# A two-layer vision block: fc1 by blocks of quarters, convolution taps cut to the image, and w1's sums kept in banks

## The chip, the cores and the metric

The kernel runs on one core of a Trainium2 chip. The metric is the device time of one execution in microseconds; the kernel before has a median of 3316.8 us in three runs (3315.48 to 3319.44). The core has a matrix engine (TensorE, PE in the profile), a vector engine (VectorE, DVE), a scalar engine (ScalarE, ACT), and GpSimd (POOL), which here mostly issues DMAs that add to memory. PE writes its results to eight banks of an accumulator memory (PSUM), each of 128 partitions by 512 fp32 numbers. DVE and ACT read them from there.

## The reference

The input is eight images of 384 channels by 32 x 32 points, all in fp32. Two layers follow.

```python
# layer 0: attention and MLP over the 1024 points of an image
xn = layernorm(x); q, k, v = split(xn @ w_qkv.T + b_qkv)
x1 = softmax(q @ k.T * SCALE) @ v @ w_proj.T + b_proj + x
h = gelu(layernorm(x1) @ w_fc1.T + b_fc1)          # 384 -> 1536: "fc1"
y = x1 + h @ w_fc2.T + b_fc2                       # 1536 -> 384: "fc2"
# layer 1: ConvNeXt block with global response normalization
z = depthwise_conv_7x7(y, dw_w, padding=3)         # 49 taps a channel
z = gelu(layernorm(z) @ w1 + b1)                   # 384 -> 1536: "up"
z = z * (1 + gamma * norm_over_points(z) / mean_over_channels(...)) + beta
out = y + z @ w2 + b2                              # 1536 -> 384: "down"
```

## The kernel before

An image is held as channels on 128 partitions, three tiles deep, by 1024 points in two halves of 512. A product is one weight tile of 128 x 128 times 512 points. The order of instructions is made by a small model of PE's time, `flow`: every product calls `flow.pe(U)` with `U = 0.857`, and chains of other work (norms, the convolution) are generators whose `yield` says after how many microseconds of PE time their next piece is emitted. The order on each engine is thus fixed when the program is built; at run time each engine goes through its own list and waits on semaphores.

Several layers already use schemes of the Strassen kind: fc2 and w2 in thirds with 15 products for 18, q/k and w1 with 11 for 12. fc1 is plain:

```python
def gelu_half(hid, m, h, xn, weights, wname, name):
    w = weights.at(wname, m // CM)[:, m % CM * CT : (m % CM + 1) * CT, :]
    ps = linear_half(lambda k: w[:, k, :], lambda k: xn[:, k, :], CT, h, f"{name}_{h}_{m}")   # 3 products
    other_table(hid[:, m, half(h)], ps, AF.Gelu, bias=bfc1[:, m : m + 1])

def mlp(...):
    for m in range(HT):                      # HT = 12 output tiles, first half of the points
        gelu_half(hid, m, 0, xn, weights, wa, f"fc1_{b}")
        if m == 3 and rest:
            rest()                           # second half of proj
            ln = flow.spawn(layernorm(xt, xn, 1, eps0, "g2", f"ln2_{b}", True, slow=slow))
            behind_ln(ln)                    # norm after the convolution of the image before
    flow.finish(ln)
    for m in range(HT):                      # second half of the points
        gelu_half(hid, m, 1, xn, weights, wa, f"fc1_{b}")
        ...
```

The convolution of image b-1 goes on while image b is in its attention and fc1. DVE makes 42 of the 49 taps of each channel tile over a padded image, always 32 x 32; ACT multiplies the other seven and POOL's DMA adds them:

```python
while min(done) < taps:
    ...
    dy, dx = divmod(i, KS)
    window = pad[:, ct, dy + y0 : dy + y1, dx : dx + W]
    dst = image(acc[:, ct, :])[:, y0:y1, :]
    nc.vector.scalar_tensor_tensor(dst, window, tap, dst, ALU.mult, ALU.add)     # L980
    ...
    yield next((early for m, early in first if n <= m), us)
```

In the last image the last convolution has nothing of a next image to hide in. It goes over rows in two parts, into `wqkv` (its lines are L980 too). The norms of each convolution subtract the mean (L423) from a bank that PE has filled with sums.

The w1 stage makes two output tiles at a time. Each product or pair goes into a bank of its own, and DVE adds the banks up in SBUF (L1051):

```python
nc.scalar.copy(c21, product((a11, b11)))
plus(c11, product((a13, b31), (a12, b21)), c21)
accumulate(p5, [(s1, t1)])
plus(c21, product((s2, t2)), c21)
plus(c12, p5, c21)
plus(c12, product((s4, b22), (a13, b32)), c12)
finish(i)                                    # gelu
plus(c21, product((s3, t3)), c21)
plus(c22, p5, c21)
plus(c21, product((a23, b31), (a22, t4)), c21)
plus(c22, product((a23, b32)), c22)
```

The sums of weights that these schemes need are made once, beside image 0, by a chain `prepare`: POOL's queue loads blocks into the tile that is later `acc`, DVE adds them, POOL's queue stores the forms in HBM. The same queue carries the folds of the norms (L388), by which half of the partitions are added to the other half before PE sums the rest (L394).

Of the kernel before, what the change touches and what calls it, by code (L numbers as in the profile page):

```python
# [51 lines left out]
P = 128  # L52
# [12 lines left out]
CM = 2  # L65
NC = HT // CM
U = 0.857
HELPED = 7
SCALE = HD ** -0.5
EPS0, EPS1, GRN_EPS = 1e-5, 1e-6, 1e-6  # L70
# [81 lines left out]
def block_kernel(  # L152
# [25 lines left out]
    flow = Flow()  # L178
    quiet = []
    s_fc2 = dram.tile([P, len(FORMS), 4 * P], F32, tag="s_fc2", bufs=1, name="s_fc2")  # L180
    s_w2 = dram.tile([P, len(FORMS), 4 * P], F32, tag="s_w2", bufs=1, name="s_w2")
    s_qk = dram.tile([P, CT, 4 * P], F32, tag="s_qk", bufs=1, name="s_qk")
    s_w1 = dram.tile([P, HT // 2, 4, P], F32, tag="s_w1", bufs=1, name="s_w1")

    def half(h):
        return slice(h * NH, (h + 1) * NH)
# [106 lines left out]

    RAW = ("A11", "A12", "A21", "A22", "A31", "A32")

    def plan_fc1(tag):
        return [((f"fc1_{tag}", c), chunk(wfc1, c)) for c in range(NC)]

    def plan_fc2(tag):
        return [((f"fc2_{tag}", a), chunk(wfc2, c)) for c, a in enumerate(RAW)]  # L300
# [491 lines left out]
    def add_first(xt, r, n, bank):  # L792
        dst = xt[:, r, half(n)]
        nc.vector.scalar_tensor_tensor(dst, bank, col("bfc2", r), dst, ALU.add, ALU.add)  # L794

    def mlp(b, xt, xn, weights, tag, ln, rest, before_fc2=None, behind_ln=None):

        hid = one.tile([P, HT * N], F32, tag="big", name=f"hid_{b}").rearrange("p (m n) -> p m n", m=HT)
        e = [three.tile([P, 2, NH], F32, tag="p", name=f"fc2_e_{b}_{i}") for i in range(2)]
        wa = f"fc1_{tag}"  # L800
        flow.finish(ln)
        for m in range(HT):
            gelu_half(hid, m, 0, xn, weights, wa, f"fc1_{b}")
            if m == 3 and rest:
                rest()
                slow = 1.2 if b == 1 else 1.0
                ln = flow.spawn(layernorm(xt, xn, 1, eps0, "g2", f"ln2_{b}", True, slow=slow))
                behind_ln(ln)
        flow.finish(ln)
        for m in range(HT):  # L810
            gelu_half(hid, m, 1, xn, weights, wa, f"fc1_{b}")
            if m % CM == CM - 1:
                weights.used(wa, m // CM)
            if m in (3, 5):
                two_tiles = hid[:, m - 3 : m - 1, :]
                difference(e[(m - 3) // 2], two_tiles[:, :, half(0)], two_tiles[:, :, half(1)])
        if before_fc2:
            before_fc2()
        bias = lambda r: col("bfc2", r)
        by_thirds(xt, hid, e, True, weights, f"fc2_{tag}", bias, lambda r, n: pad_half(xt, r, n), f"fc2_{b}")  # L820
# [132 lines left out]
    def keep(b, xt):  # L953
# [2 lines left out]
        nc.sync.dma_start(out=kept.rearrange("(c p) n -> p c n", p=P), in_=xt)  # L956
        return kept

    def convolution(acc, us, first=(), y0=0, y1=H, ready=tuple(range(CT)), taken=None):

        done = [0] * CT
        ct, n = None, 0
        taps = KS * KS - (HELPED if taken is not None else 0)
        while min(done) < taps:
            left = [c for c in ready if done[c] < taps and not (taken and taken.get(c, 0) > flow.now)]
            if not left:
                yield 1.0
                continue  # L970
            ct = min([c for c in left if c != ct] or left, key=lambda c: done[c])
            i = done[ct]
            dy, dx = divmod(i, KS)
            window = pad[:, ct, dy + y0 : dy + y1, dx : dx + W]
            dst = image(acc[:, ct, :])[:, y0:y1, :]
            tap = col("dww", ct * KS * KS + i)
            if i == 0:
                nc.vector.tensor_scalar(dst, window, tap, col("dwb", ct), ALU.mult, ALU.add)  # L978
            else:
                nc.vector.scalar_tensor_tensor(dst, window, tap, dst, ALU.mult, ALU.add)  # L980
            done[ct] += 1
            n += 1
            yield next((early for m, early in first if n <= m), us)

    def help_convolution(acc, us, taken):

        yield 8.0
        for ct in reversed(range(CT)):
            taken[ct] = float("inf")
            for i in range(KS * KS - HELPED, KS * KS):  # L990
                dy, dx = divmod(i, KS)
                for h in range(2):
                    if quiet:
                        while quiet:
                            yield 1.0
                        yield 3.0
                    t = three.tile([P, NH], F32, tag="res", bufs=4, name=f"tap_{ct}_{i}_{h}")
                    y0 = dy + h * H // 2
                    window = pad[:, ct, y0 : y0 + H // 2, dx : dx + W]
                    tap = col("dww", ct * KS * KS + i)  # L1000
                    nc.scalar.mul(t.rearrange("p (h w) -> p h w", w=W), window, tap)  # L1001
                    nc.gpsimd.dma_start(out=acc[:, ct, half(h)], in_=t, accum_op=ALU.add)  # L1002
                    yield us
            taken[ct] = flow.now + 8.0
        yield 8.0
        taken.clear()
# [10 lines left out]
    def grn_up(b, acc, weights, tag):  # L1017
# [7 lines left out]
        wa = f"w1_{tag}"  # L1025
        spent = {}

        def finish(m):
            other_table(y[:, m, :], y[:, m, :], AF.Gelu, bias=b1[:, m : m + 1])

        def squares(i):
            for m in (i, i + HT // 2):
# [3 lines left out]
        for i in range(HT // 2):  # L1036
            j = i + HT // 2
            raw, sums = weights.at(wa, i, "A"), weights.at(wa, i, "S")
            a11, a12, a13, a22, a23 = (raw[:, k, :] for k in range(5))
            s1, s2, s3, s4 = (sums[:, k, :] for k in range(4))  # L1040
            spent[i] = ps_s.tile([P, 2, NH], F32, tag="s", name=f"h_{b}_{i}_5")
            p5 = spent[i][:, 0, :]
            c11, c12, c21, c22 = (y[:, m, half(n)] for m in (i, j) for n in range(2))

            def product(*pairs):
                bank = o_tile(f"h_{b}_{i}")
                accumulate(bank, list(pairs))
                return bank

            def plus(dst, bank, part):  # L1050
                nc.vector.tensor_tensor(dst, bank, part, ALU.add)  # L1051

            nc.scalar.copy(c21, product((a11, b11)))
            if i:
                finish(j - 1)
                squares(i - 1)
            plus(c11, product((a13, b31), (a12, b21)), c21)
            accumulate(p5, [(s1, t1)])
            plus(c21, product((s2, t2)), c21)
            plus(c12, p5, c21)  # L1060
            plus(c12, product((s4, b22), (a13, b32)), c12)
            finish(i)
            plus(c21, product((s3, t3)), c21)
            plus(c22, p5, c21)
            plus(c21, product((a23, b31), (a22, t4)), c21)
            plus(c22, product((a23, b32)), c22)
            for part in ("A", "S"):
                weights.used(wa, i, part)
        finish(HT - 1)
        squares(HT // 2 - 1)  # L1070
        return y, gx
# [189 lines left out]
    def prepare(weights, aside):  # L1261
# [17 lines left out]
        def load_blocks(w, name, *which):  # L1279
            t = one.tile([P, CT, N], F32, tag="acc", name=name).rearrange("p c n -> p (c n)")  # L1280
            parts = []
            for j, (m, k) in enumerate(which):
                parts.append(t[:, j * 4 * P : (j + 1) * 4 * P])
                nc.gpsimd.dma_start(out=parts[j], in_=block_of(w, m, k))
            return parts

        def spare(name):
            return three.tile([P, NH], F32, tag="res", bufs=4, name=name)
# [5 lines left out]
            nc.vector.tensor_tensor(dst, x, y, ALU.add)  # L1294

        def forms(name, w, store):
            def keep_form(i, t):
                nc.gpsimd.dma_start(out=store[:, i, :], in_=t)

            a11, a12, a31, a33, a13, a23 = load_blocks(w, f"{name}_a", (1, 1), (1, 2), (3, 1), (3, 3), (1, 3), (2, 3))  # L1300
            x, y, z = (spare(f"{name}_{k}") for k in "xyz")
            yield 16.0
            add(a23, a23, a33)
            add(a11, a11, a12)
# [17 lines left out]
            keep_form(12, a12)  # L1322
            nc.vector.tensor_scalar(a23, a23, -1.0, None, ALU.mult)
            keep_form(14, a23)
            a21, a22, a31, a32, a33, a12 = load_blocks(w, f"{name}_b", (2, 1), (2, 2), (3, 1), (3, 2), (3, 3), (1, 2))
            x, y = spare(f"{name}_v"), spare(f"{name}_w")
            nc.gpsimd.dma_start(out=x, in_=block_of(w, 2, 3))
            yield 25.0
            add(x, x, a33)
            sub(y, a22, x)  # L1330
            keep_form(7, y)
# [70 lines left out]
        yield 4.0  # L1402
        for j, key in enumerate(order):
            nc.gpsimd.dma_start(out=s_w1[:, :, int(key[1]) - 1, :], in_=t[:, j])
        yield from shift_through_w2()
        yield from forms("w2", w2, s_w2)

    def first_values(xn):

# [10 lines left out]
    def main():  # L1420
# [17 lines left out]
        plan = plan_fc1(0) + plan_fc2_fast(0) + plan_qk(1)  # L1438
        for b in range(1, B):
            if b < B - 1:  # L1440
                plan += plan_fc1(b) + plan_fc2_fast(b)
            else:
                for h in range(2):
                    plan += plan_fc1(f"{b}_{h}") + plan_fc2(f"{b}_{h}")
# [80 lines left out]
        for b in range(B):  # L1525
# [22 lines left out]
            flow.finish(state["norm3"])  # L1548
            if b < B - 1:
                y, gx = grn_up(b - 1, acc, weights, b - 1)  # L1550
                start_conv(b, 1.65 if b == B - 2 else 1.7, (26, 2.2), (27, 9.0), (35, 4.4))
                scale = flow.spawn(grn_scale(b - 1, gx, weights, b - 1, y))
                next_values(b + 1)
                flow.finish(scale)
# [166 lines left out]
```

## Time and profile before

| | us | share of 3315.9 |
|---|---|---|
| PE busy | 3279.8 | 99% |
| DVE busy | 2511.5 | 76% |
| ACT busy | 1604.1 | 48% |
| POOL busy | 484.2 | 15% |
| first product of `v` starts | 16.5 | |
| image 3: attention and proj | 1169.1 to 1296.3 | |
| image 3: fc1 | 1296.2 to 1367.8 | |
| image 3: fc2 | 1368.7 to 1421.6 | |
| image 2's w1 | 1421.5 to 1480.7 | |

An image takes 400 us in the middle of the run. In the profile, a line such as `L351 PE MATMUL fc<-xn,fc 128*128 128x512 f32 x1152 | 504.0, 596` is a group: its line in the kernel, engine and operation, the tile written and those read, the shape, the count, and the busy time and mean ns of one. Each fp32 product is two records, so 1152 records are 576 products. After the second bar stands idle time of the engine just before the group and what ended most of it. In the list of waits a row names the engine and line that waited, the one waited for, and total, times and longest. In a timeline the first number is the start, the second the length, and the bracket the idle time before it.

### The profile page before, as it was taken

The page shows a single profiled execution, that of the slowest core. Times are in us where ns is not written, and L with a number is a line of the kernel's source. Part 1 is how long each engine was busy: PE and PEld are TensorE (multiplying, and loading weights), DVE is VectorE, ACT ScalarE, POOL GpSimd, SP SyncE. Part 2 cuts the span into 40 slices and gives each one's busy share as a digit, 9 for nine tenths or more (in the row PEclk, how much of TensorE's full clock was granted, in tenths as well). Part 3 has the DMA queues.
Part 4 walks back from the last instruction along what each step waited for, and adds up shares of the span by engine and source line. Part 5 has one row for each costly group of instructions (what it writes and reads, how often), then busy time and mean ns, then how long its engine had stood idle before and what let it go on. Part 6 is the DMA issues. An engine that isn't in the chain of part 4 may idle for free. (4 is left out here: it accounts for less than half of the span.)

```text
span 3315.9 us, 38765 instructions
## 1 busy us (share of the span) xinstructions
PE 3279.8 (99%) x14296; PEld 1415.0 (43%) x14296; DVE 2511.5 (76%) x3186; ACT 1604.1 (48%) x2194; POOL 484.2 (15%) x569
## 2 busy tenths in 40 slices
PE   8999999999999999999999999999999999999998
PEld 4344434443344433444344443444434443444455
DVE  4444897888867978679786798768886888879940
ACT  2542663447534375353652737526473355623541
POOL 2121210112110121101211022111220112100000
PEclk9999999999999999999999999999999999999999
DMA  5336732657244563537436373273742647333231
GB/s 197 112 106 147 150 68 71 156 115 150 56 104 135 137 127 58 131 106 172 84 58 148 103 187 70 58 179 84 175 78 50 180 106 160 63 74 89 69 95 43
DMA packets 199109, 368.73 MB, mean 111 GB/s; under 512 B 40768, under 2 KB 46784, under 8 KB 198528
## 3 DMA queue, kind: packets, MB, share of 16 engines
q0 software_dynamic: 80896, 158.63, 26.3%
q1 hardware_dynamic: 117728, 206.83, 20.7%
q8 instruction: 115, 1.88, 0.2%
q10 hardware_dynamic: 288, 0.71, 0.1%
q14 instruction: 82, 0.67, 0.1%
HBM read 187.03 MB, written 34.60 MB: 67 GB/s over the span
## 5 line engine op out<-in xcount | busy, mean ns | idle before, releaser
L980 DVE SCALAR_TENSOR_TENSOR acc<-pad,vec,acc 128x1024 f32<-128x1024 f32 x861 | 1069.3, 1276 | 20.1 <-DMA acc<-tap 15.5
L673 ACT ACTIVATE p<-s 128x1024 f32<-128x1024 f32 x512 | 523.8, 1023 | 278.5 <-PE s L664 270.1
L664 PE MATMUL s<-qk 48*64 48x512 f32 x4096 | 544.7, 593 | 0.8 <-ACT p L673 0.6
L684 PE MATMUL o<-p,v 64*64 64x512 f32 x4096 | 541.2, 591 | 0.0
L351 PE MATMUL fc<-xn,fc 128*128 128x512 f32 x1152 | 504.0, 596 | 4.8 <-DVE acc L423 4.8
L1002 POOL DMA_DIRECT2D acc<-tap x294 | 253.7, 884 | 1212.2 <-ACT tap L1001 747.9
L351 PEld LDWEIGHTS fc<-xn,fc 128*128 128x128 f32 x1152 | 219.2, 191 | 285.6 <-issue 275.7
L358 PE MATMUL fc_p<-hid,fc 128*128 128x512 f32 x728 | 318.6, 594 | 0.2 <-DMA hid<-hid 0.2
L370 ACT ACTIVATE hid<-fc,bfc_f 128x512 f32<-128x512 f32 x192 | 131.5, 686 | 348.0 <-PE fc L351 347.6
L684 PEld LDWEIGHTS o<-p,v 64*64 64x64 f32 x4096 | 165.5, 133 | 278.3 <-issue 266.7
L664 PEld LDWEIGHTS s<-qk 48*64 48x64 f32 x4096 | 161.2, 133 | 278.6 <-issue 220.5
L358 PE MATMUL o_p<-y,w 128*128 128x512 f32 x624 | 272.3, 593 | 0.0
L1051 DVE TENSOR_TENSOR y<-h,y 128x512 f32<-128x512 f32 x288 | 197.0, 690 | 90.8 <-PE h L358 76.2
L1001 ACT ACTIVATE tap<-pad,vec 128x512 f32<-128x512 f32 x294 | 210.9, 727 | 25.4 <-DMA acc<-tap 25.2
L358 PEld LDWEIGHTS fc_p<-hid,fc 128*128 128x128 f32 x728 | 137.2, 190 | 179.0 <-issue 166.5
L358 PE MATMUL h<-acc,w_A 128*128 128x512 f32 x432 | 207.3, 595 | 0.0
L980 DVE SCALAR_TENSOR_TENSOR wqkv<-pad,vec,wqkv 128x416 f32<-128x416 f32 (+1 forms) x288 | 193.5, 744 | 0.5
L358 PEld LDWEIGHTS o_p<-y,w 128*128 128x128 f32 x624 | 117.5, 190 | 150.6 <-issue 129.1
L790 ACT COPY pad<-x 128x512 f32<-128x512 f32 x48 | 30.2, 635 | 251.0 <-DVE x L856 187.0
L625 DVE TENSOR_TENSOR attn<-o,attn 128x512 f32<-128x512 f32 x64 | 44.1, 689 | 138.6 <-ACT attn L623 138.6
L549 DVE TENSOR_TENSOR qk<-qk,qk 128x512 f32<-128x512 f32 x168 | 111.5, 686 | 29.0 <-PE qk L358 20.0
L592 PE MATMUL v<-wqkv,xn 128*128 128x384 f32 x384 | 128.2, 491 | 0.0
(311 smaller groups left out, 3751.4 us busy)
## 6 DMA issues: line engine op xcount, KB each, us to landing
acc<-tap POOLq DMA_DIRECT2D x294, 256.0 KB, 3.5
w_A<-in_w SPq DMA_DIRECT2D x72, 384.0 KB
fc<-s_fc SPq DMA_DIRECT2D x91, 256.0 KB
hid<-hid POOLq DMA_DIRECT2D x42, 512.0 KB, 7.1
fc<-in_wfc SPq DMA_DIRECT2D x54, 384.0 KB
w<-s_w SPq DMA_DIRECT2D x78, 256.0 KB
y<-y POOLq DMA_DIRECT2D x36, 512.0 KB, 6.8
kept<-x SPq DMA_DIRECT2D x8, 1536.0 KB
```

The lines of the kernel that those rows point to most:

```text
L351: nc.tensor.matmul(out=ps, lhsT=lhsT(k), rhs=rhs(k)[:, half(h)], start=(k == 0), stop=(k == nk - 1))
L358: nc.tensor.matmul(out=bank, lhsT=lhsT, rhs=rhs, start=k == 0, stop=k == len(pairs) - 1)
L370: nc.scalar.activation(dst, src, function, **kw)
L549: nc.vector.tensor_tensor(dst, bank, part, ALU.add)
L592: nc.tensor.matmul(out=ps[:, :C], lhsT=xn[:, k, t * P : (t + 1) * P], rhs=wv_sb[:, k, :], start=(k == 0), stop=(k == CT - 1),)
L664: nc.tensor.matmul(out=s[64 * i : 64 * i + 64, j, :], lhsT=kT[64 * j : 64 * j + HD, m, k0 : k0 + 64], rhs=qT[64 * j : 64 * j + HD, m, half ...
L673: nc.scalar.activation(p, s, AF.Exp)
L684: nc.tensor.matmul(out=outs[i][64 * j : 64 * j + 64, :], lhsT=v[keys, t, at : at + 64], rhs=p[keys, j, :], start=(t == 0), stop=(t == KT - 1),
L980: nc.vector.scalar_tensor_tensor(dst, window, tap, dst, ALU.mult, ALU.add)
L1001: nc.scalar.mul(t.rearrange("p (h w) -> p h w", w=W), window, tap)
L1002: nc.gpsimd.dma_start(out=acc[:, ct, half(h)], in_=t, accum_op=ALU.add)
L1051: nc.vector.tensor_tensor(dst, bank, part, ALU.add)
```

## The change

It does four things.

- fc1, images 1 to 6, second half of the points: the tiles 6 to 11 are made in two groups of three, each as a product of a 3 x 3 block of weights and a 3 x 2 block of points (quarters of 256), with 15 products of 256 points in place of 9 of 512. It takes ten sums of quarters of `xn` per image, and 15 forms of the weights per group, made once in `prepare` and loaded with the other weights. To make room the tiles 6 to 11 come first in the first half.
- Some of the additions are left to PE: a product is added to a bank (`start=False`) after DVE or ACT has read what the bank held before.
- The w1 stage is rewritten in the same manner, with a fifth sum of weights: 11 products as before, five DVE additions for eight, and ACT's gelu reads one bank directly.
- A convolution tap covers only the points for which it reaches inside the image. The taps' order is changed so that the seven in ACT's share are those of the middle column, and the pace of the convolution is set anew.

```diff
+    def fc1_group(hid, group, xn, sums, weights, wname, name, late):
+        ...
+        y = product(6, bank("y"))
+        nc.scalar.copy(c11, y)
+        t = product(2, bank("t"))
+        nc.scalar.mul(c21, t, -1.0)
+        x = product(0, bank("x", True))
+        nc.scalar.copy(n16, x)
+        z = product(10, bank("z"))
+        product(5, y, True)              # True: added to what the bank holds
+        lately()
+        product(1, t, True)
+        op(n16, y, n16)                  # op: a DVE addition of 128 x 256
+        x = product(3, bank("u", True))
+        op(c32, x, n16)
+        v_ = product(12, bank("v"))
+        nc.scalar.copy(c12, v_)
+        op(c32, c32, z, ALU.subtract)
+        x = product(4, bank("w", True))
+        lately()
+        op(n17, x, n16)
+        op(c31, t, n17)
+        op(c12, c12, z, ALU.subtract)
+        product(13, y, True)
+        lately()
+        product(11, v_, True)
+        op(c12, y, c12)
+        x = product(14, bank("q", True))
+        op(c11, v_, c11)
+        product(9, v_, True)
+        op(c21, x, c21)
+        product(7, z, True)
+        product(8, x, True)
+        op(n17, v_, n17, ALU.subtract)
+        op(c22, z, n17)
+        op(c21, c21, n17)
+        op(c11, x, c11)
 ...
     def mlp(...):
+        if fast:                                     # images 1 to 6
+            flow.finish(making)                      # the ten sums of quarters
+            plain(0)
+            plain(1)
+            late.append(lambda: difference_of(0))
+            fc1_group(hid, 0, ...)
+            plain(2)
+            fc1_group(hid, 1, ...)
+            plain(3)
+            difference_of(1)
+            for m in (4, 5):
+                plain(m)
+                late.pop(0)()
+            late.pop(0)()
 ...
     def convolution(...):
-            window = pad[:, ct, dy + y0 : dy + y1, dx : dx + W]
-            dst = image(acc[:, ct, :])[:, y0:y1, :]
+            rows, cols = inside(dy, dx, y0, y1)
+            window = inner(ct)[:, rows.start + dy - PAD : ..., cols.start + dx - PAD : ...]
+            dst = image(acc[:, ct, :])[:, rows, cols]
-            yield next((early for m, early in first if n <= m), us)
+            yield share * next((early for m, early in first if n <= m), us)
 ...
     def grn_up(...):
+            first = products(o_tile(f"h_{b}_{i}_1"), (a11, b11))
+            nc.scalar.copy(c21, first)
+            second = products(o_tile(f"h_{b}_{i}_2"), (s2, t2))
+            plus(c21, second, c21)
+            ...
+            third = products(o_tile(f"h_{b}_{i}_3"), (s3, t3))
+            plus(c22, third, c21)
+            fifth = products(spent[i][:, 0, :], (s1, t1), (a23, b32))
+            plus(c22, fifth, c22)
+            products(first, (a12, b21), (a13, b31), more=True)
+            finish(i, half(0), first)
+            products(fifth, (s4, b22), (s5, b32), more=True)
+            plus(c12, fifth, c21)
+            products(third, (a23, b31), (a22, t4), more=True)
+            plus(c21, third, c21)
 ...
     def prepare(...):                                # after the forms of w2
+        yield from forms("fc1", wfc1, s_fc1)         # 15 forms of 128 x 256
 ...
-                start_conv(b, 1.65 if b == B - 2 else 1.7, (26, 2.2), (27, 9.0), (35, 4.4))
+                start_conv(b, 1.55 if b == B - 2 else 1.58, (26, 2.1), (27, 9.0), (35, 4.4))
```

## The prediction

> **What bounds the kernel now.** I read four views in this order: the page's first part, its groups of instructions, the list of what TensorE (PE) waited for, and the timelines of single stages.
>
> ```profile
> PE 3279.8 (99%) x14296; PEld 1415.0 (43%) x14296; DVE 2511.5 (76%) x3186; ACT 1604.1 (48%) x2194; POOL 484.2 (15%) x569
> ...
> L980 DVE SCALAR_TENSOR_TENSOR acc<-pad,vec,acc 128x1024 f32<-128x1024 f32 x861 | 1069.3, 1276 | 20.1 <-DMA acc<-tap 15.5
> ...
> L351 PE MATMUL fc<-xn,fc 128*128 128x512 f32 x1152 | 504.0, 596 | 4.8 <-DVE acc L423 4.8
> ...
> L1051 DVE TENSOR_TENSOR y<-h,y 128x512 f32<-128x512 f32 x288 | 197.0, 690 | 90.8 <-PE h L358 76.2
> ```
>
> PE is busy 99% of 3315.9 us. A busy PE could still be a slow one, so I divided: 1152 records of fc1 in 504.0 us are 0.4375 us each, and 576 products of 512 columns are two records each, so 0.86 us a product in a stream, launch to launch. The timeline of an undisturbed stage gives the same. PE therefore has next to no slack, and only two things can shorten the run: fewer products, or the few waits. VectorE (DVE) at 76% costs time only where PE waits for it:
>
> ```profile
> PE ln_sum L380 <- DVE ln_a L416: 11.8, 5, 5.9
> PE fc L351 <- DVE acc L423: 4.8, 1, 4.8
> PE ln_var L380 <- DVE ln_sq L437: 2.4, 1, 2.4
> PE h_last L1150 <- DVE wqkv L451: 1.6, 1, 1.6
> PE ln_var L394 <- DMA ln_sq<-ln_sq: 1.2, 2, 1.0
> ```
>
> The first row is almost all the start (10.1 us of it before the first products), the third and fourth lie after the last convolution, where a norm has no product beside it. The second row is the one the change can reach. It is in the last image, at 2979 us:
>
> ```profile
> 2971.65 2.74 PE L351 MATMUL fc<-xn,fc 128*128 128x512 f32 x6
> 2979.20 11.03 PE L351 MATMUL fc<-xn,fc 128*128 128x512 f32 x18 [4.81 <-DVE acc L423]
> ```
>
> The stretch after it, by the view of windows:
>
> ```profile
> 2979.00:2983.00 4.00, 3.81 (x5) 1.77 (x6) 4.00 (x8) 2.50 (x5) 0.00 (x0) 0.50 0.00 0
> 2983.00:2987.00 4.00, 4.00 (x7) 1.55 (x7) 3.30 (x7) 2.06 (x3) 0.00 (x0) 0.70 0.30 77
> ```
>
> After the width stand five engines' busy times (PE, weight loads, DVE, ACT, POOL), and then PE's granted clock: 0.50 and 0.70. PE waited 4.8 us and then ran eight records at half speed, 0.43 us lost on each: 3.4 us more. The wait's true price is 8.2 us.
>
> [...] The trace agrees (4.81 us idle, then clock 0.50; waits of 1 to 2.5 us elsewhere cost no such stretch). [...] the trace's 128x256 scalar_tensor_tensor takes 412, and 331 start to start. [...] The new banks "that go on as sums" rest on it; nothing in the kernel before does this, so no trace here shows its cost.
>
> **The change, part by part.**
>
> *Quarters in fc1.* In images 1 to 6, two groups of three output tiles are made for the second half of the columns with 15 products of 256 columns instead of 9 of 512: 7.5 against 9 units of 0.86 us. Saved: 1.5 x 0.86 = 1.29 us a group, 12 groups, **15.5 us**. [...]
>
> Against that stand waits, because a bank is read by DVE or ScalarE (ACT) and then written by PE again. Take a group's first product as 0. The bank y is complete at 2.15 us, and DVE sees it 0.2 us after the last pass (PE to DVE is 630 ns from the start of a last 512-column pass of 429). From there eight additions follow in DVE's order until the read of bank v that product 9 waits for. At 0.33 us each, with 0.1 us more for those that use the result just before, and with banks u and w not there before 3.2 and 4.1 us, they end near 6.1 us. PE would reach product 9 at 5.16. So a group waits about 1.0 us by its own chain.
>
> The built program shows what stands between these additions. In images 2 to 6 the first group has one convolution tap after its third addition and another after its eighth; the second group has none. A tap takes 1.196 us now (start to start); inside the image its mean is 30.3 x 30 pixels, 910/1024 of the columns, so 0.95 + 0.13 = 1.08 us. The first tap falls wholly on the chain, the second by about half. An image then waits 1.0 + 1.0 + 1.6 = 3.6 us and saves 2.6. Image 1 has two or three taps in each group: some 5 us. Full count of waits: 5 x 3.6 + 5 = 23 us. I take 14, since latencies may overlap better than in this serial count, and the changed pacing numbers look tuned to it. Net: **-1.5 us**.
>
> *Taps inside the image.* 126 taps an image lose 0.12 us each, 15 us of DVE; the ten quarter sums and 26 additions put back 36 x 0.36 = 13. DVE's share hardly falls in fc1, and a DVE that is off the path pays nothing. It pays at 2979 us. There DVE ran 12 taps without a break while PE worked on:
>
> ```profile
> 2936.72 15.81 DVE L980 SCALAR_TENSOR_TENSOR acc<-pad,vec,acc 128x1024 f32<-128x1024 f32 x12 [1.72 <-DMA acc<-tap]
> 2952.45 2.07 DVE L451 SCALAR_TENSOR_TENSOR xn<-xn,vec,ln_rstd 128x512 f32<-128x512 f32 x3
> ```
>
> In the changed program 10 stand there: 10.8 us for 15.8. The shorter taps of the last convolution, 0.51 for 0.57 us, give 2 us more. The subtraction L423 would then end near 2972 to 2974 instead of 2979, and PE wants the bank at 2974.4. The 4.8 us and the slow clock go: **-8 us**. In the same image PE's wait of 1.0 us for the fold of `ln_sq` (L394, fifth row above) stands behind a DVE that is full of taps: **-1 us**.
>
> *w1's blocks.* 11 products before, 11 after; additions 8 to 5, 11 us less DVE an image (18 x 0.6). PE had no wait in that stage (59 us for 66 products at 0.86 plus the norm's sums). The new order reads the bank `fifth` 0.8 us before PE returns to it. Worth **0**.
>
> *Preparation.* Forms of fc1 and s5 are made once, in image 0, by DVE and by POOL's DMA queue. No product is added. But the built order on POOL puts three stores of forms ahead of the fold of `ln_sq`, and the third waits for DVE additions which come after it. Before, the fold was issued as soon as DVE was ready, and PE wanted its result almost at once:
>
> ```profile
> 312.09 0.85 POOL L388 DMA_DIRECT2D ln_sq<-ln_sq  x1 [6.42 <-DVE ln_sq L437]
> ```
>
> ```profile
> 315.50 1.07 PE L394 MATMUL ln_var<-ln_sq,ones 64*64 64x512 f32 x4 [0.17 <-DMA ln_sq<-ln_sq]
> ```
>
> The fold would be issued near 316.5, so PE waits about 4 us, and may run slow after it. I put it at **+3 us**, since the additions may have been done earlier than I place them.
>
> Sum: -1.5 - 8 - 1 + 0 + 3 = -7.5, so 3316.8 becomes about 3309.
>
> **Rivals.** *The waits in fc1 eat more than the products save.* For: the serial count of 23 us against 15.5, the taps in the order, and image 1. Against: DVE idles about 20 us late in fc1 in the trace before (19.1 us before L423 in image 3), so the time for the additions is there; only their place is wrong. With the preparation's wait in full it makes 3322 to 3328. *All products are saved and nothing waits.* For: waits of this kind nearly don't occur in the kernel before, whose order was evidently tuned. Against: there no product waits for a chain of eight additions. It makes 3316.8 - 15.5 - 9 = 3292. *DVE's relief shows nowhere:* the last image finds another wait (ACT's pad copies, 0.7 us each, or the helper's DMA that released the 12 taps). Then the 8 us stay: 3317.
>
> **Range and chances.** The rivals' ends are 3292 and 3328, and I take 3293 to 3328. Two per cent is 66 us; every product saved and every wait of PE removed is 15.5 + 25 = 41. Slower by 66 us would need a slow clock in all twelve groups and more. Hence 0.02, 0.96, 0.02.
>
> **What would show it.** Of PE's records 18 of 512 columns make way for 30 of 256 in each group, so the count rises by 144 while fc1, 71.5 us long in image 3, should shrink by 2.6 if nothing waits; if it shrinks by under 1 or grows, the first rival is right, and PE's waits must name DVE `hid` in the line of the group's products. L423's 4.8 us should be gone and the clock 1.00 near 2970. In image 0, PE's wait for `ln_sq` should grow to 3 us or more. The w1 stage should keep its 59 us. I am wrong in kind if the waits list names a weight load's DMA or ACT above these.

## The result: 3339.7 us, slower by 0.7%

The changed kernel took 3339.7 us (median of 4, 3339.2 to 3344.2), the kernel before beside it 3317.4. The ratio is 1.007, 95% interval 1.0053 to 1.0088. The prediction of 3309 with a range up to 3328 was wrong.

TensorE (PE) does less and waits more. The page's first part, after (before: PE 3279.8 of 3315.9 us, DVE 2511.5):

```profile
span 3337.6 us, 39409 instructions
PE 3272.0 (98%) x14440; PEld 1437.8 (43%) x14440; DVE 2409.3 (72%) x3315; ACT 1627.2 (49%) x2278; POOL 507.6 (15%) x600
```

The 144 additional records are there and PE is busy 8 us less, in a span 22 us longer. The first rows of what PE waited for, after (us in total, times, longest):

```profile
PE fc_v L838 <- DVE hid L843: 18.5, 12, 2.5
PE ln_sum L390 <- DVE ln_a L426: 12.2, 6, 6.1
PE ln_sum L404 <- DMA ln_a<-ln_a: 7.1, 1, 7.1
PE h L1196 <- DVE y L1203: 6.3, 8, 0.9
PE ln_var L404 <- DMA ln_sq<-ln_sq: 6.2, 2, 5.0
```

Four of the five rows are new or larger (the second is the start, as before): the groups of fc1, once in each of the 12; two folds in image 0; and w1's new order, 8 times in six images. The wait of 4.8 us for `acc` in the last image is gone, and the window of that stretch shows PE busy throughout at clock 1.00:

```profile
2971.00:3012.00 41.00, 41.00 (x102) 17.42 (x100) 38.62 (x60) 8.20 (x13) 1.63 (x2) 1.00 0.32 82
```

A list of waits doesn't give their price, so I cut both traces, and later those of the experiments, into stages by the first product of each. Each time is worked out from two starts in the timeline, in us, "fc1" up to the start of fc2, for images 2 to 6 the mean:

```
stage                   before  after    e1     e2     e3     e6     e7    e11
image 0, fc1              71.4   72.4   71.4   71.4   72.1   72.0   71.9   73.0
image 0, fc2              57.2   72.3   57.4   58.7   58.9   73.7   73.6   57.3
image 1, fc1              71.4   74.8   71.4   78.0   71.4   72.2   70.7   71.0
image 1, w1               59.3   62.4   59.3   59.3   63.0   62.4   62.4   59.3
images 2 to 6, fc1        72.5   74.6   72.6   75.5   72.6   71.6   70.7   70.7
images 2 to 6, w1         59.1   60.2   59.1   59.1   60.2   60.2   60.2   59.1
last image, fc1 2nd half  40.2   32.3   32.3   32.3   32.3   32.3   32.4   32.3
```

After minus before, in us: image 0's fc2 +15.1; fc1 of images 1 to 6 +14.2 (3.4 in image 1, 10.8 in the five others); w1 +8.7 (3.1 + 5 x 1.1); fc1 of image 0 +1.0. Against it the last image's fc1 -7.9, the two last stages (the last image's up and its end) -2.9, and -6.6 in small gains (attention -4.2, fc2 elsewhere -1.0, w2 -1.4). That makes +21.6 of the spans' +21.7. The expected 15 us of products did not go to one new bound. Each part brought its own wait.

**The group of quarters, image 3.** PE's timeline of the first group (start, duration, engine, line, output <- inputs, idle before it and what ended it):

```profile
1365.08 0.59 PE L838 MATMUL fc_y<-fc_t,fc1f 128*128 128x256 f32 x2
...
1369.83 0.59 PE L838 MATMUL fc_q<-hid,fc1f 128*128 128x256 f32 x2
1372.28 0.70 PE L838 MATMUL fc_v<-hid,fc1f 128*128 128x256 f32 x2 [1.86 <-DVE hid L843]
1372.82 0.59 PE L838 MATMUL fc_z<-hid,fc1f 128*128 128x256 f32 x2
1373.65 0.70 PE L838 MATMUL fc_q<-xn,fc1f 128*128 128x256 f32 x2 [0.24 <-DVE hid L843]
1374.18 2.74 PE L361 MATMUL fc<-xn,fc 128*128 128x512 f32 x6
```

Twelve products run 0.43 us apart. The thirteenth adds into `v` and must wait until VectorE (DVE) has read `v`. DVE's timeline shows why that is late:

```profile
1367.51 0.42 DVE L843 TENSOR_TENSOR fc_n<-fc_y,fc_n 128x256 f32<-128x256 f32 x1 [1.57 <-PE fc_y L838]
...
1369.10 1.15 DVE L1129 SCALAR_TENSOR_TENSOR acc<-pad,vec,acc 128x899 f32<-128x899 f32 x1
...
1371.81 0.41 DVE L843 TENSOR_TENSOR hid<-fc_v,hid 128x256 f32<-128x256 f32 x1
```

The read of `v` is the last line, eighth addition of the group, with a tap in the middle. The group took 9.10 us, start to next product, where 9 products of 512 columns take 7.71 (9 times 0.857). The second group, without a tap, waited 0.87 and took 7.61, hardly less than the 7.71 that it replaces.

**What the same wait costs elsewhere.** In images 2, 4 and 5 the stage is 1.3 us longer than in 3 and 6, after the same wait of 1.86 us and without the one of 0.24 us that follows it there. The view of windows, 7 us from the end of that wait on, image 2 and then image 3:

```profile
969.00:976.00 7.00, 6.93 (x18) 4.18 (x19) 6.57 (x12) 1.00 (x3) 0.86 (x1) 0.76 0.48 116
1372.20:1379.20 7.00, 6.68 (x24) 4.46 (x25) 6.51 (x13) 2.19 (x5) 0.85 (x1) 1.00 0.47 116
```

The granted clock is the third figure from the right: 0.76 against 1.00, 18 records against 24. Image 2 lost 1.25 us on image 3 although it waited once less. With that wait and its restart (0.24 and 0.26 us, see below) added, the slow stretch cost some 1.7 us in each of the three images.

**Image 0.** The timeline of GpSimd (POOL), after: the loads of fc1's second set of blocks stand ahead of the mean's fold (`ln_a`), the store of `fc_w` ahead of that of the squares (`ln_sq`):

```profile
286.05 4.33 POOL L1450 DMA_DIRECT2D fc_b<-in_wfc  x6 [6.33 <-DMA s_fc<-fc_a]
...
292.59 1.91 POOL L398 DMA_DIRECT2D ln_a<-ln_a  x1
...
322.10 0.71 POOL L1467 DMA_DIRECT2D s_fc<-fc_w  x1 [7.89 <-DVE fc_w L1456]
...
323.45 1.04 POOL L398 DMA_DIRECT2D ln_sq<-ln_sq  x1
```

And PE's:

```profile
302.89 1.97 PE L404 MATMUL ln_sum<-ln_a,ones 64*64 64x512 f32 x4 [7.09 <-DMA ln_a<-ln_a]
...
328.16 1.12 PE L404 MATMUL ln_var<-ln_sq,ones 64*64 64x512 f32 x2 [5.04 <-DMA ln_sq<-ln_sq]
```

The mean's fold was issued 3.7 us later than before (288.85 then) and took 10.3 us to PE instead of 8.0. The squares' fold was ready at 318.84, when DVE ended, and was issued 4.6 us after that. Price: 6.4 and 4.9 us more waiting, and 4.1 us in all for slow records after the two waits (PE busy 60.9 us in this stretch for the work of 56.8; the clock was 0.50 from 301 to 305 us and again from 329 to 333).

### The profile page after: what moved, and what is told of

The parts are those of the page before. It is cut to its first block, busy times and chain, and to the rows that moved or that the text cites. A ratio compares the mean times of both kernels' runs of the same rounds, so it can differ in the third digit from the quotient of the medians.

```text
span 3337.6 us, 39409 instructions
## 1 busy us (share of the span) xinstructions
PE 3272.0 (98%) x14440; PEld 1437.8 (43%) x14440; DVE 2409.3 (72%) x3315; ACT 1627.2 (49%) x2278; POOL 507.6 (15%) x600
## 4 chain that ended last, share of the span: by engine, by line
PE 95%; DVE 2%; DMA 1%; issue 1%; ACT 0%; POOL 0%; SPq 0%; DVEq 0%; POOLq 0%; ACTq 0%
PE fc L361 13%; PE s L674 13%; PE o L694 13%; PE fc_p L368 11%; PE h L1196 10%; PE o_p L368 9%; PE qk L368 6%; PE v L602 4%; PE o L1263 4%; PE proj L616 3%; PE h_last L1307 2%; PE h L348 2%; PE qk L348 1%; DVE hid L843 1%; PE ln_sum L404 1%
## 5 line engine op out<-in xcount | busy, mean ns | idle before, releaser
L1129 DVE SCALAR_TENSOR_TENSOR acc<-pad,vec,acc 128x899 f32<-128x899 f32 (+8 forms) x861 | 962.8, 1155 | 6.2 <-DMA acc<-tap 3.1
L361 PE MATMUL fc<-xn,fc 128*128 128x512 f32 x936 | 414.0, 597 | 0.0
L380 ACT ACTIVATE hid<-fc,bfc_f 128x512 f32<-128x512 f32 x156 | 106.6, 687 | 346.7 <-PE fc L361 346.6
L361 PEld LDWEIGHTS fc<-xn,fc 128*128 128x128 f32 x936 | 177.7, 191 | 225.1 <-issue 209.4
L1203 DVE TENSOR_TENSOR y<-h,y 128x512 f32<-128x512 f32 x180 | 124.3, 690 | 161.1 <-PE h L1196 150.7
L1129 DVE SCALAR_TENSOR_TENSOR wqkv<-pad,vec,wqkv 128x377 f32<-128x377 f32 (+24 forms) x288 | 177.3, 689 | 0.6
L1196 PE MATMUL h<-acc,w_A 128*128 128x512 f32 x360 | 172.9, 594 | 0.0
```

Of the source, the lines that this page charges most:

```text
L361: nc.tensor.matmul(out=ps, lhsT=lhsT(k), rhs=rhs(k)[:, half(h)], start=(k == 0), stop=(k == nk - 1))
L1196: nc.tensor.matmul(out=bank, lhsT=lhsT, rhs=rhs, start=not more and k == 0, stop=True, skip_group_check=more or k > 0)
```

## Experiments

Each kernel was timed beside the kernel before (medians there 3316 to 3317). The theory at first: three causes that have nothing to do with each other, namely the place of one addition and of taps in a group, the place of fc1's blocks on POOL's queue, and w1's order.

**e1, taps alone.** The kernel before, with the new `convolution` and its pace, nothing else.

> The kernel before with only the convolution changed (taps inside the image, new pace). Theory: the stages of the changed kernel add up, and the taps' part is what its last image and its other attention stages gained: fc1's second half 40.2 to 32.3, last up block 41.2 to 39.9, end 11.3 to 9.6, about 0.3 in each of five images, together 13 to 14 us: 3304 (3301 to 3307). Rival: the gain in the last image came from another part, so the stage keeps 40 us: 3313 to 3318.

3303.5 us, ratio 0.9963 (0.9949 to 0.9976). The last image's fc1 fell to 32.3. The end stage stayed at 11.3, so that gain of the changed kernel isn't the taps'.

**e2, w1's stage of before** (the edit in words).

```
-  t = blocks("w1_sums_b"); load blocks 2, 4; yield 14; subtract; store s5
-  grn_up with banks that go on
+  grn_up of before (8 additions, a bank for each sum)
```

> The changed kernel with the w1 stage of before and without the fifth sum in the preparation. Theory: the w1 stage goes from 62.4 and 60.2 back to 59.2 us in all six images (8.7 us), and as the preparation is then some 15 us ahead, the folds of image 0 are issued before fc1's blocks and its fc2 goes from 72.3 to 57 to 60 us: 3316 to 3320. Rival A: w1's stage is longer because of the convolution's new pace or the layer norm beside it: the stage stays near 60 us. Rival B: image 0's loss does not come from the place of the preparation in time: fc2 of image 0 stays near 72 and the time is 3331.

3322.7 us, ratio 1.002 (1.0012 to 1.0028). w1 is back at 59.3 and 59.1 us, so rival A falls. Image 0's fc2 took 58.7 with the preparation 15 us ahead, so rival B falls. The time missed the range because fc1 became longer, 78.0 and 75.5 us. Its waits hardly changed (19.6 us in all against 19.0); in the changed kernel only three of the images 2 to 6 had taken 75 us and here all five did. The clock differed: after the same wait of 2.24 us in image 1, the changed kernel and then e2:

```profile
563.70:570.70 7.00, 6.96 (x26) 5.04 (x27) 6.64 (x10) 2.24 (x5) 0.00 (x0) 1.00 0.41 102
550.40:557.40 7.00, 6.99 (x19) 4.22 (x20) 6.19 (x9) 1.11 (x3) 0.00 (x0) 0.76 0.39 101
```

After that image's second wait, of 2.52 us, it was 1.00 and 0.76 again.

**e3, fc1 plain.**

```
-  fast = FAST if isinstance(b, int) and b > 0 else 0
+  fast = 0
-  yield from forms("fc1", wfc1, s_fc1)
```

> The changed kernel with fc1 plain everywhere and none of its blocks prepared; taps and w1 stage as changed. Theory: fc1 of images 1 to 6 goes back to 71.4 to 72.5 us (14 us), image 0's fc2 to about 57 (15 us), its fc1 to 71.4 (1 us): 3309 to 3312. Rival: vector engine's load, not the groups, makes the waits; then the relief from taking the groups out shows only in part, fc1 stays above 73 us, 3318 or more.

3309.5 us, ratio 0.998 (0.9971 to 0.9988), as the theory had it. The groups and the preparation of their blocks are 30.2 us of the changed kernel's time; w1's 60.2 and 63.0 us stayed.

**e4, loads 24 us later.** One line ahead of the second set of loads: `if w is wfc1: yield 24.0`.

> The changed kernel with the second set of fc1's blocks loaded 24 us later in the preparation, so that on GpSimd's queue the fold of the mean stands ahead of these loads, and the fold of the squares ahead of the stores; all else equal, the same bytes move. Theory (place in the queue): TensorE's wait for the mean's fold falls from 7.1 to about 1 us, that for the squares' from 5.0 to below 1, the slow clock after each is gone, fc2 of image 0 takes 58 to 61 us, 3326 to 3329. Rival (the transfers themselves fill the DMA engines): the folds are late still, fc2 of image 0 stays above 68 us, 3335 or more.

3337.6 us, ratio 1.0066 (1.0052 to 1.0079); fc2 of image 0 63.3 us. POOL's timeline, and PE's below it:

```profile
288.36 1.35 POOL L398 DMA_DIRECT2D ln_a<-ln_a  x1
...
305.09 4.84 POOL L1450 DMA_DIRECT2D fc_b<-in_wfc  x6
...
313.07 0.89 POOL L398 DMA_DIRECT2D ln_sq<-ln_sq  x1 [2.42 <-DMA hid<-hid]
```

```profile
296.62 1.08 PE L404 MATMUL ln_sum<-ln_a,ones 64*64 64x512 f32 x4 [1.00 <-DMA ln_a<-ln_a]
...
318.81 1.97 PE L404 MATMUL ln_var<-ln_sq,ones 64*64 64x512 f32 x4 [3.59 <-DMA ln_sq<-ln_sq]
```

Half the expectation came true. The mean's fold, ahead of the loads now, cost 1.0 us instead of 7.1 while the DMA engines were no less full (share 0.98 from 285 to 300 us, 0.85 in the changed kernel): the place in the queue, not the traffic, had held it. The squares' fold now had the seven loads just ahead of it and took 5.7 us to PE. The loads' late stores also ran into image 1's convolution, whose tile they share: DVE waited 5.9 us for them before its first taps, PE then 2.3 us for DVE, and the next attention took 4.3 us more. The loss was moved rather than removed.

**e5, taps held.** `flow.inside = True` while a group is issued, so that no tap or norm step comes between its additions.

> The changed kernel with the convolution's taps and the layer norm's steps held back while a group of fc1's quarters is issued; they run after it. Theory (the group's own chain of additions costs 0.9 us a group, and each tap inside one another 1.1): the first group's wait falls from 1.9 to 0.9 us in images 2 to 6, some clock losses go with it, but the held taps delay the second group by about 1 us: fc1 of images 2 to 6 at 73 to 75 us, 3330 to 3338. Rival (the wait is the taps' alone): no wait for fc_v in the first group.

3356.8 us, ratio 1.0126 (1.0111 to 1.0142), worse than expected. The first group did wait 0.87 us, as much as the second had without taps, so a tap on the chain is worth 1.0 us and the group's own chain 0.87. But the held steps ran in one burst between the groups (DVE, then PE, image 3):

```profile
1374.08 5.79 DVE L1133 SCALAR_TENSOR_TENSOR acc<-pad,vec,acc 128x870 f32<-128x870 f32 x5
...
1382.57 0.42 DVE L843 TENSOR_TENSOR fc_n<-fc_y,fc_n 128x256 f32<-128x256 f32 x1
```

```profile
1383.04 1.20 PE L838 MATMUL fc_y<-xn,fc1f 128*128 128x256 f32 x2 [3.21 <-DVE fc_n L843]
```

Five taps and four steps of the norm, 8.5 us, met one output of 2.6 us between the groups; the second group's first addition came late and PE waited 3.2 us. I had expected a delay of about 1 us. That is not the whole loss. fc1 and fc2 together took 2.0 us more in each of the images 2 to 6 than in the changed kernel, and w1 took 61.5 us instead of 60.2: the norm's sums fell elsewhere in it, and PE waited there 0.85 us twice an image instead of once (10.6 us in all against 6.3).

**e6, another order in the group.** The same 15 products and 13 additions:

```
-  products  6 2 0 10 5 1 3 12 4 13 11 14 9 7 8      read of v: 8th addition
+  products  6 12 0 5 11 2 10 3 1 9 14 4 13 7 8      read of v: 2nd addition
```

> The changed kernel with the same 15 products and 13 additions of a group in another order: the two products of v come early, the addition that reads v between them is the second one and no longer the eighth, and its last product stands six places after. Taps stay where the schedule puts them. Theory (the place of that addition in VectorE's order is the cause): fc_v's wait is gone, what is left is what a tap inside pushes (0 to 1 us in the first group of an image): fc1 of images 2 to 6 at 70 to 72 us instead of 73.8 to 75.3, 3312 to 3322. Rival (VectorE has too much to do in a group whatever the order): the waits move to z and q with the same total, 3333 or more.

3322.3 us, ratio 1.0018 (1.0011 to 1.0024); fc1 71.6 us in all of images 2 to 6. The wait for `v` is gone (0.3 us in all). What remains is 0.9 us once an image, after the first group, where two taps stand among the additions and the next output needs a bank. VectorE was not overloaded; one addition had the wrong place.

**e7, order, hold and room.** e6's order, the steps held as in e5, and outputs 2 to 4 (three, not the four that the expectation names) between the groups instead of 2 alone. Outputs 3 and 4 are then written over quarter sums that the second group still reads, so its outputs 9 to 11 are made of other numbers than the reference's; the instructions are the same in number and size.

> The order of the last kernel, the steps held back during a group, and four plain outputs between the two groups instead of one, so that the held taps have room. Theory: no waits in groups, fc1 of images 2 to 6 at 70 us (72.5 less twice 1.27), of image 1 at 69 to 70: 3309 to 3315. Rival (products of 256 columns don't run at half the time of 512): fc1 stays above 71.5 us without any wait.

3316.5 us, ratio 0.9999 (0.9991 to 1.0007), fc1 70.7. The whole first group in image 3, and the output after it:

```profile
1358.52 0.59 PE L838 MATMUL fc_y<-fc_t,fc1f 128*128 128x256 f32 x2
...
1365.01 7.89 PE L361 MATMUL fc<-xn,fc 128*128 128x512 f32 x18
```

6.49 us instead of 7.71, without a wait: the products of 256 columns do save 1.22 us a group, against the predicted 1.29. The second group took 7.10, as PE waited 0.36 us for ACT's copy of `y`, once in each of the six images. That is why the stage takes 70.7 us and not 70, and the time lies just above its range.

**e8, e7 with e2.** As in e7, outputs 9 to 11 are made of other numbers than the reference's.

> e7 with the w1 stage of before and without its fifth sum in the preparation (as in e2). Theory: the parts add up: before 3316 less 13 for the taps, less 15 for fc1, plus 1 to 3 in image 0: 3288 to 3293. Rival: parts share a resource, so that the sum is missed by 5 us or more: above 3298.

3296.9 us, ratio 0.9942 (0.9928 to 0.9956). The sum was missed by 4 to 9 us, most of it in image 0: fc2 62.8 us, with a wait of 3.5 us for the squares' fold, which took 6.2 us to PE where e2's, in the same order, took 4.2. The parts add up; image 0 doesn't keep still.

**e9, the third sum of w1 in another bank.** `third = products(spent[i][:, 1, :], (s3, t3))`.

> The changed kernel with the third running sum of a w1 block in the unused half of the block's large PSUM tile instead of one of the four small banks. Theory (banks: two sums that go on and the two folded sums of the layer norm hold all four small banks, so the third sum waits until the second product has been read): TensorE's wait for y is gone or below 1 us in total, the w1 stage takes 59.1 to 59.4 us in all six images, 3329 to 3333. Rival (VectorE's queue: the layer norm's subtractions delay the addition that is read): the waits stay, 3337 or more.

3422.7 us, ratio 1.0321 (1.0307 to 1.0335). Theory and rival both expected far less. PE's wait for DVE in w1 came to 65.5 us, in 72 times. 72 is two for each of the 36 blocks: the first product of the fifth sum waits until the third has been read, and the third goes on only after the fifth has been read. The two sums lie in different banks but in one tile of the program. This fits waits that are kept for the tile as a whole; the run does not answer the question it was made for.

**e10, e7 with the sums kept.** Four sums go into the tile of the second difference, two into output 5; the second difference (of two halves of `hid`, which fc2 uses) is made after the second group.

> As e7, but four of the quarter sums lie in the tile of the second difference, and two in output 5, so that outputs 2 to 4 may stand between the groups without overwriting sums that the second group still reads; the second difference is made after the second group. Theory: the same instructions as in e7, fc1 of images 2 to 6 at 70.7 us, of image 1 at 70 to 71; 3314 to 3319. Rival: the later difference makes fc2 wait, fc2 above 53.5 us instead of 52.7, 3321 or more.

3318.1 us, ratio 1.0003 (0.9995 to 1.0012), fc1 70.7 in images 1 to 6. So e7's time holds for the full computation. The later difference cost 1.3 us in image 1's fc2 (55.3) and nothing in the others.

**e11, everything together.** e10 with w1's stage of before, and the preparation shortened: the parts 0 and 1 of w2's shift (a vector that the preparation sums from w2's blocks) are loaded together, with one `yield 14.0` for two.

> e10 with the w1 stage of before, without the fifth sum, and with two of the three parts of w2's shift loaded together in the preparation, so that fc1's blocks come some 18 us earlier and all their stores are issued before the mean's fold. Theory: image 0's fc2 falls from 62.8 (e8) to 57.5 to 60 us, the rest as in e8: 3289 to 3295. Rival (the added transfers fill the DMA engines wherever they are): fc2 of image 0 stays at 62 or moves its loss into fc1 or attention of image 0; 3296 or more.

3300.1 us, ratio 0.9952 (0.9938 to 0.9965): the whole computation, 16 us faster than before and 40 faster than the changed kernel. Against e1's 0.9963 the intervals overlap, so e11 is not shown to be faster than taps alone. POOL's timeline:

```profile
269.65 0.69 POOL L1464 DMA_DIRECT2D s_fc<-fc_b  x1 [2.06 <-DVE fc_b L1456]
...
291.30 1.33 POOL L398 DMA_DIRECT2D ln_a<-ln_a  x1
...
314.73 0.84 POOL L398 DMA_DIRECT2D ln_sq<-ln_sq  x1 [6.51 <-DVE ln_sq L447]
```

The last store of fc1's blocks is issued 20 us before the first fold, and image 0's fc2 takes 57.3 us, as it did before. It missed its range by 5 us. Attention of image 0 took 1.3 us more than in e8 and its fc1 1.7 (PE waited 1.9 us there for the shift's sum and 1.3 for `attn`), and image 1's fc2 57.7, where the two folds' waits came to 1.0 us (0.65 and 0.33) and a slower clock followed, 0.52 from 584 to 586 us.

**e12, e11 with e9's w1 stage.**

> e11, but with the new w1 stage of e9 (third sum in the large tile) and the fifth sum prepared. Theory: three additions fewer in each block relieve VectorE where TensorE is the bound, so the w1 stage takes 59.1 to 59.4 us as in e11; the fifth sum's load costs nothing or up to 4 us in image 0: 3290 to 3298. Rival (VectorE's relief is worth something beside the norm): the stage falls below 58.5 us and the time below e11's by 3 or more.

3386.4 us, ratio 1.0212 (1.0198 to 1.0226). It has e9's 72 waits again (66.2 us), and w1's stage takes 72.6 to 76.7 us. It tells nothing more of w1's worth.

**e13, the third sum later.** In the changed kernel:

```
-  third = products(o_tile(...), (s3, t3)); plus(c22, third, c21)
-  fifth = products(spent[i][:, 0, :], (s1, t1), (a23, b32))
+  fifth = products(spent[i][:, 0, :], (s1, t1), (a23, b32))
+  third = products(o_tile(...), (s3, t3)); plus(c22, third, c21)
```

> The changed kernel with the third running sum of a w1 block started after the two first products of the fifth, that is 1.7 us later; same banks, same additions. Theory (banks: in the block after the norm's fold the third sum needs the bank that the second product still holds until VectorE has read it, 0.9 us): by the later place the bank is free, the waits are gone in images 2 to 6, the w1 stage takes 59.1 us there and 59.1 to 60.5 in image 1: 3330 to 3334. Rival (the fold's subtractions on VectorE delay what TensorE needs, wherever the product stands): a wait of 0.5 us or more stays in each image, stage 59.9 or more, 3336 or more.

The stage did nearly as the theory had it: PE's wait fell from 6.3 to 0.5 us in all, the stage from 60.2 to 59.4 in images 2 to 6 and from 62.4 to 60.9 in image 1. The place where the changed kernel had waited, PE and then DVE, image 3:

```profile
1457.55 1.02 PE L1196 MATMUL h<-attn,w_S 128*128 128x512 f32 x2
1459.42 1.99 PE L1196 MATMUL h<-attn,w_S 128*128 128x512 f32 x4 [0.85 <-DVE y L1203]
```

```profile
1456.69 1.29 DVE L433 SCALAR_TENSOR_TENSOR xn<-ln_sum,xn 128x512 f32<-128x512 f32 x2 [0.32 <-PE ln_sum L404]
1458.67 0.69 DVE L1203 TENSOR_TENSOR y<-h,y 128x512 f32<-128x512 f32 x1 [0.70 <-PE h L1196]
```

DVE read the second product 0.1 us after it was complete and had idled before; the norm's subtractions had not held it up. The third sum waited for that read, in images 2 to 6 only in the block after the norm's sums, whose two small banks were still in use beside those of the first sum and the second product; in other blocks it didn't wait. e5 agrees: there both of the norm's sums stand ahead of a block's second product, and PE waited 0.85 us after each, while in the changed kernel the sums of the squares stand behind it (at 1478.50 us, the product at 1477.55) and nothing waits. That the bank is the reason rests on this count of four; that the place of the third sum decides is shown. The whole run took 3340.6 us, ratio 1.0071 (1.0058 to 1.0085), no less than the changed kernel: image 1's fc1 took 78.1 us instead of 74.8 and image 0's fc2 73.3 instead of 72.3. Stages, not totals, had to be compared here.

**e14, e11 mended.** 6 us instead of 4 between the parts of the shift; image 1's taps at 1.56 instead of 1.6.

> e11 with 6 us instead of 4 between the parts of w2's shift in the preparation, and image 1's taps paced 2.5% closer. Theory: the waits for the shift in image 0's attention (1.9 and 1.3 us, and the clock after them) go, and image 1's fold comes before its fc2: 3293 to 3298. Rival: the waits only move: 3299 or more.

3304.4 us, ratio 0.9959 (0.9946 to 0.9973). The mending cost more than it saved: the first set of blocks was loaded 7 us later and the second, behind other transfers on the queue, 22 us later; the last stores waited 5.0 us for DVE, up to 296.4 us, and the mean's fold behind them was issued at 300.0. Image 0's attention took 2.9 us more than in e11 and its fc2 68.4 us. Image 1's fc2 fell to 55.5.

**e15, e14 with e13's w1 stage.**

> e14 with the new w1 stage in the order of e13 and the fifth sum prepared. Theory (TensorE is the bound in this stage, VectorE's relief is worth nothing): w1 stage 59.1 us as in e14, image 0 up to 4 us longer as the preparation is longer: e14 plus 0 to 5. Rival: e14 less 2 or more.

3310.2 us, ratio 0.9981 (0.9973 to 0.999). The stage takes 59.4 us instead of 59.1, in image 1 60.9 instead of 59.3, together 3.3 of the 5.9 us above e14 (0 to 5 expected). Five additions for eight are worth nothing here, even when the order doesn't wait.

## Why the prediction was wrong, point by point

- **Products saved, 15.5 us:** right in kind and nearly in size, 1.22 us a group where nothing waits (e7), 14.6 us for twelve. No wait names a weight load: they took 190 ns, beside passes of 256 columns 0.215 us apart (two to a product of 0.43 us). The 504.0 us over 576 products are 0.875 us, not 0.86; 0.86 is the distance in the stream, and nothing hangs on the difference.
- **Waits in the groups: "Full count of waits: ... 23 us. I take 14".** This step failed. The chain was right: 0.87 us by the group's own additions (predicted 1.0), 1.0 more in the first group with taps (predicted 1.6), 4.8 in image 1 (predicted 5). The list has 19.0 us. The discount "since latencies may overlap better" had no measurement behind it. And a wait was priced at its idle time: from fc1's +14.2 and the 14.6 saved, the groups lost 28.8 us. Of the 9.8 beyond the idle, some 5.2 are the slow clock in three images (1.7 to 1.75 each). In image 3's first group, starting again took 0.26 us a wait (9.10 - 6.49 - 2.10 idle, for two; the second group, 7.61 - 6.49 - 0.87, gives 0.25). At that rate the 14 waits make 3.6, and about 1.0 stays unassigned. The prediction had priced the one wait of 4.8 us with its slow clock, and took waits of 1 to 2.5 us to have none; the trace before says otherwise (last section). This was my first rival, with the right sign and too narrow an end.
- **Preparation, +3 us:** this step failed by the most, 15.1. The squares' fold was nearly as worked out (5.0 us of wait against "about 4"), but I discounted it and gave the slow clock after it nothing. The term left out is the mean's fold: the built order has seven loads ahead of it too, and I counted only the stores ahead of `ln_sq`. e4 shows the queue as its cause, e11 that blocks which come early cost image 0's fc2 nothing.
- **w1's blocks, 0:** this step failed, 8.7 us. I reckoned with the bank `fifth`, which has its 0.8 us, and not with how many banks are open at once: PE waited 0.85 us for the third sum, and e13 moves it away. Two sums that go on, one product and two folded sums want five small banks, and there are four (argued, not shown). That the five additions save nothing was right (e15).
- **Taps: -8 us, and the wait of 1.0 for `ln_sq`, -1 us.** The first was right: 7.9, clock 1.00, and e1 has it alone. The second was not: a wait of 1.1 us is left in the last image.
- **Not foreseen:** gains of 2.9 us in the two last stages and 6.6 in small ones. e1 has most of the small ones; the end stage varied from 7.6 to 11.3 us among these kernels, and I have no cause for it.
- **The range:** its upper end was one rival alone, and that rival's 3322 to 3328 does not come out of its terms. With the full count in fc1 (9 us more) and the preparation as worked out (4 instead of 3) they make 3319; 3340 needed the three things left out: the mean's fold, the open banks and the price of a wait beyond its idle time.

## What to carry to other kernels

Where TensorE is 99% busy, a change that saves products is worth what its order lets through: look for each read of a bank that a product goes on writing, count what stands ahead of it on the reading engine, and move that read rather than make the engine faster. Count the banks open at once at the worst moment, with the neighbours' sums, and count everything on a shared DMA queue ahead of a short transfer on the critical path. When holding work back, count the burst that follows, and compare stage by stage: two single edits here (e4, e13) did what they were made for and the total hid it.

## What the runs showed of the hardware that I had not expected

A slow clock followed waits of 1.86 and 2.24 us here, but not each time. A wait of 1.86 us was followed by 0.76 over the next 7 us in image 2 and by 1.00 in image 3, with the same order of products; one of 2.24 us in image 1 by 1.00 in the changed kernel and by 0.76 in e2. Why equal waits differ, no run here shows. The trace before already had a slow clock beside short waits. Between 3183 and 3191 us PE waits 1.70, 2.45 and 1.62 us, each time for DVE and here close together, and the clock is 0.50:

```profile
3188.00:3192.00 4.00, 2.38 (x5) 1.26 (x6) 1.72 (x4) 2.68 (x4) 0.00 (x0) 0.50 0.00 0
3192.00:3196.00 4.00, 4.00 (x10) 2.82 (x9) 0.55 (x2) 1.04 (x3) 0.00 (x0) 0.50 0.00 0
```

So the prediction's line that waits of 1 to 2.5 us cost no such stretch was a wrong reading; it holds at the start (1.00 from 9 to 20 us, around waits of 1.97 and 1.10 us), not here.

Banks that go on as sums after a read cost no time in these runs where the read was done before PE returned: the first group of e7 ran 15 products into eight sums, five of them read and then continued, in 6.49 us without a wait. In its second group one such read, ACT's of `y`, was late, and PE waited 0.36 us.
